# Turning the relative-value sums of an attention layer inside SBUF instead of over DRAM and TensorE

## The chip, the cores and the metric

The kernel runs on one core of a Trainium2 chip. The time is the device time of one execution in microseconds (us). Before the change it is 2808.07 us, the median of 3 runs (2802.43 to 2817.08). Engines are named as the profile names them: PE (TensorE matmuls) and PEld (its weight loads), DVE (VectorE), ACT (ScalarE), POOL (GpSimd), and SP, the engine that issues most DMAs. L875 is line 875 of the kernel.

## What is computed

Two layers act on x (64 batches, 128 rows, 128 columns), each with cross-attention to a context of 77 rows per batch and a mixture of 8 experts. The change touches the attention of layer 1, which has 16 heads of 8 columns and learned relative positions. Cut to what matters:

```python
scores = einsum('bhqd,bhkd->bhqk', q, k) + einsum('bhqd,qkd->bhqk', q, rel_key_table[ids])
attn   = softmax(scores / sqrt(8))
out    = einsum('bhqk,bhkd->bhqd', attn, v)
out    = out + einsum('bhqk,qkd->bhqd', attn, rel_value_table[ids])   # the relative values' sums
x      = x + tanh(g) * (out.reshape(B, S, H) @ Wo + bo)
# then the experts: x = x + tanh(g') * sum_e combine[e] * relu(x @ W1[e])**2 @ W2[e]
```

The second addend of `out` has a matrix of its own for every row q, since `rel_value_table[ids]` depends on q and k. The kernel therefore computes it for one q at a time, over all heads and batches of a group together. This leaves the sums with the 8 columns d on partitions, while everything else of `out` has the rows q on partitions. The sums must be turned before they can be added.

## The kernel before

**Stages.** Layer 0 comes first, then layer 1. Layer 1 works through 16 groups of 4 batches. Group 0 is done as two halves of 2 batches (nb = 2), the other 15 with nb = 4. `run` makes one step for each group, in which several generators are woven together by `weave`:

- `l1_project` (prj1) for the next group: loads x and the context (L692, L694), normalises x in place (L109 to L119, tile xg), transposes it (px, L703), projects q, k, v (L710, L712) and sends q and k through DRAM (dq and dk out at L141 and L146, qst and kst back at L726 and L738).
- `l1_relate` (rel1) for the next group: 256 small matmuls (L770), copied out by ACT (L776), written to DRAM as ra (L777) and read back in another layout as rq (L790).
- `l1_attend` (att1) for this group: 16 units, each with 4 score matmuls (L815), the addition of rq (L817, DVE), the row maximum (L818, DVE), its subtraction (L819, POOL), 4 transposes (L827), the exponential into the tile rel (L828, ACT) and 4 matmuls with the values (L835). Every four units a batch's result is turned by four PE transposes (L845) and copied into avt, with q on partitions (L846). After the units, 128 matmuls for the relative values (L875, two instructions each in the trace) fill four PSUM banks, each copied to rvs (L879, DVE).
- `l1_out` (out1) for the group before: completes `out` and multiplies it with Wo (L907, L909, L913, L915).
- the route (L929 to L953) and a share of the experts, `tape`, which fills the rest of the step: per expert 12 matmuls into pz (helper lines L156 to L158), Relu, square, a split in two parts (ACT L979 to L986, DVE L981, POOL L987), and 6 matmuls into py. Before each py the expert's weights are spread over the partitions by a matmul into pb (L599), which shares one PSUM bank with py. DVE reads py at L610 or L613 (tile ys) and frees that bank; L614 adds ys to acc, on DVE or on POOL.

**Where the change is.** At the end of `l1_attend`, rvs holds, for each block j of 32 partitions, 8 columns d on the first 8 partitions, and (head, batch, 32 rows q) along the free dimension. Four DMAs write it to DRAM as rd (L883) and one reads it back as rp with (d, head) on partitions and (batch, q) free (L885). In `l1_out` PE transposes rp (L899, one for each batch, PSUM tile po1), DVE adds it to avt (L901), DVE takes the reciprocal of the denominators (L902), and POOL multiplies (L903). Then come the transposes po2 (L907).

**What sets the order.** `PLAN` gives each generator a stretch of its step, from 0 to about 1, and some a priority; the number of parts given with the generator spreads its parts over that stretch. The compiler's scheduler then reorders the instructions of each engine by its own estimate of when they can run. On the chip each engine runs its list strictly in that order, so a waiting instruction holds up everything behind it on its engine. rvs and rp share one buffer (tag rvs), and av, o1 and oT share two (tag av).

Of the kernel before, what the change touches and what calls it, by code (L numbers as in the profile page):

```python
# [10 lines left out]
F32 = mybir.dt.float32  # L11
# [3 lines left out]
ALU = mybir.AluOpType  # L15
# [4 lines left out]
B, S, D = 64, 128, 128  # L20
KL = 77
NH = 16
HD = 8
# [18 lines left out]
def weave(tc, streams):  # L42
# [20 lines left out]
PLAN = dict(  # L63
    out=(0, 0.2, 2000),
    wei=(0, 0.7, 0),
    max=(0.2, 0.95, 1000),
    fea=(0.2, 0.6, 1000),
    out1=(0.25, 0.4, 600),
    att1=(0.1, 0.95, 0),
    rel1=(0.37, 0.93, 0),  # L70
    relT=(0.6, 0.9, 500),
# [4 lines left out]
    attE=(0, 0.35, 500),  # L76
    tE=(0.1, 1.1, 0),
    prjT=(0, 0.55, 1000),
    attL=(0.1, 0.4, 500),
# [16 lines left out]
class Net:  # L96
# [695 lines left out]
        s["rqs"][b] = rq.rearrange("q (j g) k -> q g j k", j=4)  # L792

    def l1_attend(self, s, nb):
        nc, a, dp = self.nc, self.ap, self.dp
        qst, kst, va = s["qst"], s["kst"], s["va"]
        C = NH * nb
        nq = 512 // C

        rel = self.rel  # L800
        rqs = s["rqs"]


        avt = a.tile([128, nb, NH, HD + 1], F32, tag="avt", bufs=2, name="avt")
        relg = rel.rearrange("k q (j g) b e -> k g b j q e", j=4)

        def scores(b, hg):

            m = a.tile([128, 4], F32, tag="mx", bufs=3, name="mx")
            sc = a.tile([128, 4, KL], F32, tag="sc", bufs=2, name="sc")  # L810
            r = slice(64 * (b // 2), 64 * (b // 2) + 48)
            sp = self.sbank().rearrange("p (j k) -> p j k", j=4)
            for j in range(4):
                h = 4 * j + hg
                nc.tensor.matmul(sp[:, j, :KL], lhsT=qst[r, h, b % 2, :], rhs=kst[r, h, b % 2, :], start=True, stop=True,  # L815
                                 tile_position=(r.start, 0))
            nc.vector.tensor_tensor(sc, sp[:, :, :KL], rqs[b][:, hg], ALU.add)  # L817
            nc.vector.tensor_reduce(m, sc, AX.X, ALU.max)  # L818
            nc.gpsimd.tensor_tensor(sc, sc, m.unsqueeze(2).to_broadcast([128, 4, KL]), ALU.subtract)  # L819
            return sc  # L820

        def expo(b, hg, sc):
            st = self.pST.tile([128, 4, 128], F32, tag="ST", name="ST")
            for j in range(4):

                r = 128 if j < 3 else KL
                nc.tensor.transpose(st[:r, j, :], sc.rearrange("q j k -> q (j k)")[:, j * KL : j * KL + r], self.ident)  # L827
            nc.scalar.activation(relg[:KL, hg, b], st[:KL].rearrange("k j (q e) -> k j q e", e=2), AF.Exp,  # L828
                                 scale=1.0 / math.sqrt(HD))

        def weigh(b, hg):
            for j in range(4):

                n = (b * NH + 4 * j + hg) * (HD + 1)
                nc.tensor.matmul(self.avp[32 * j : 32 * j + 32, hg, :], lhsT=va[:, n : n + 32],  # L835
                                 rhs=relg[:, hg, b, j, :], start=True, stop=True, tile_position=(0, 32 * j))
            if hg == 3:
                av = a.tile([128, 4, S], F32, tag="av", bufs=2, name="av")
                nc.scalar.copy(av, self.avp)
                turns.append((b, av))  # L840

        def turn(b, av):
            pt = self.sbank()
            for g in range(4):
                nc.tensor.transpose(pt[:, g * 128 : (g + 1) * 128], av[:, g, :], self.ident)  # L845
            nc.vector.tensor_copy(avt[:, b].rearrange("q (j g) r -> q g j r", j=4),  # L846
                                  pt.rearrange("q (g j r) -> q g j r", g=4, j=4)[:, :, :, : HD + 1])

        turns = []
        parts = [(b, hg) for b in range(nb) for hg in range(4)]  # L850
        sc = {}
        ahead = self.rqb - 1
        for b in range(len(rqs), min(nb, ahead)):
            self.l1_fetch(s, b)
        for n in range(len(parts) + 2):
            if n % 4 == 0 and ahead <= n // 4 + ahead < nb:
                self.l1_fetch(s, n // 4 + ahead)
            if n < len(parts):
                sc[n] = scores(*parts[n])
            if 0 <= n - 1 < len(parts):  # L860
                expo(*parts[n - 1], sc.pop(n - 1))
            if turns:
                turn(*turns.pop())
            if n >= 2:
                weigh(*parts[n - 2])
            yield
        turn(*turns.pop())

        rvs = a.tile([128, C, 32], F32, tag="rvs", bufs=1, name="rvs")
        for t0 in range(0, 32, nq):  # L870
            pr = self.sbank()
            for n in range(nq):
                for j in range(4):
                    q = 32 * j + t0 + n
                    nc.tensor.matmul(pr[32 * j : 32 * j + 32, n * C : (n + 1) * C],  # L875
                                     lhsT=self.rv[:, 127 - q : 131 - q, :].rearrange("k n d -> k (n d)"),
                                     rhs=rel[:, q // 2, :, :, q % 2], start=True, stop=True,
                                     tile_position=(0, 32 * j))
            nc.vector.tensor_copy(rvs[:, :, t0 : t0 + nq], pr.rearrange("p (n c) -> p c n", n=nq))  # L879
            yield  # L880
        rd = dp.tile([HD, C, 4, 32], F32, tag=f"rd{nb}", name="rd")
        for j in range(4):
            nc.sync.dma_start(out=rd[:, :, j, :], in_=rvs[32 * j : 32 * j + HD])  # L883
        rp = a.tile([128, nb * S], F32, tag="rvs", bufs=1, name="rp")
        nc.sync.dma_start(out=rp, in_=rd.rearrange("d (h b) j t -> (d h) (b j t)", h=NH))  # L885
        s["rp"], s["avt"] = rp, avt

    def l1_out(self, g, b0, nb, s):
        nc, pm, a = self.nc, self.pmisc, self.ap
        avt, rp = s["avt"], s["rp"]  # L890
        if b0 == 0:
            self.x3n = self.fp.tile([128, 4, 128], F32, tag="x1", bufs=3, name="x3")
        x3 = self.x3n[:, b0 : b0 + nb, :]
        nc.sync.dma_start(out=x3, in_=self.x2d[g, :, b0 : b0 + nb, :])
        nc.gpsimd.tensor_tensor(x3, x3, self.bo.unsqueeze(1).to_broadcast([128, nb, 128]), ALU.add)

        pt = pm.tile([128, 512], F32, tag="misc", name="po1")
        for b in range(nb):
            nc.tensor.transpose(pt[:, b * 128 : (b + 1) * 128], rp[:, b * S : (b + 1) * S], self.ident)  # L899
        o = a.tile([128, nb, NH, HD], F32, tag="av", bufs=2, name="o1")  # L900
        nc.vector.tensor_tensor(o, pt[:, : nb * 128].rearrange("q (b d h) -> q b h d", b=nb, d=HD), avt[:, :, :, :HD], ALU.add)  # L901
        nc.vector.reciprocal(avt[:, :, :, HD], avt[:, :, :, HD])  # L902
        nc.gpsimd.tensor_tensor(o, o, avt[:, :, :, HD].unsqueeze(3).to_broadcast([128, nb, NH, HD]), ALU.mult)  # L903
        yield
        pt = pm.tile([128, 512], F32, tag="misc", name="po2")
        for b in range(nb):
            nc.tensor.transpose(pt[:, b * 128 : (b + 1) * 128], o[:, b].rearrange("q h d -> q (h d)"), self.ident)  # L907
        oT = a.tile([128, nb * S], F32, tag="av", bufs=2, name="oT")
        nc.scalar.copy(oT, pt[:, : nb * S])  # L909
        yield  # L910
        pf = pm.tile([128, 512], F32, tag="misc", name="pf")
        for b in range(nb):
            nc.tensor.matmul(pf[:, b * 128 : (b + 1) * 128], lhsT=oT[:, b * S : (b + 1) * S], rhs=self.wo,  # L913
                             start=True, stop=True)
        nc.vector.scalar_tensor_tensor(x3, pf[:, : nb * 128].rearrange("p (b d) -> p b d", b=nb), self.tg[:, 1:2], x3,  # L915
                                       ALU.mult, ALU.add)
        if b0 + nb == 4:
            self.xs[self.ng + g] = self.x3n
        yield
# [124 lines left out]
    def run(self, ngroups):  # L1044
        tc, nc = self.tc, self.nc
# [26 lines left out]
        for k in range(nun + 2):  # L1072
            w = []
# [12 lines left out]
            if k == 1:  # L1086
                with tc.issue_after(self.last_dma.ins):
# [15 lines left out]
                   (self.route(ngroups - 1), 6, *PLAN["rt0"]),  # L1103
                   (self.l1_project(*h0, s1), 8, *PLAN["prjT"]),
                   (self.l1_relate(h0, s1), 7, *PLAN["relT"])], 27, PLAN["t0"])
        self.step([(self.l1_attend(s1[h0], 2), 13, *PLAN["attL"]),
                   (self.l1_project(*h1, s1), 8, *PLAN["prjL"]),
                   (self.l1_relate(h1, s1), 7, *PLAN["relL"])], self.parts(ngroups) - self.done, PLAN["t0"])
        while self.f0_open:
# [1 line left out]
        for k in range(1, ngroups + 3):  # L1111
# [12 lines left out]
                acm, self.ap = self.pool("a1", side="right")  # L1124
                self.weights(4)
            if k == 1:
                w.append((self.l1_attend(s1[h1], 2), 13, *PLAN["attL"]))
            elif k - 1 < ngroups:
                w.append((self.l1_attend(s1[k - 1, 0, 4], 4), 23, *PLAN["att1" if k < ngroups else "attE"]))
            if k < ngroups:  # L1130
                w.append((self.l1_project(k, 0, 4, s1), 8, *PLAN["prj1"]))
                w.append((self.l1_relate((k, 0, 4), s1), 13, *PLAN["rel1"]))
# [114 lines left out]
```

## Time and profile before

| what | value |
|---|---|
| median of 3 runs | 2808.07 us |
| the profiled execution's own time | 2834.67 us |
| its span | 2833.0 us |
| mean granted PE clock | 0.936 |
| busy PE / PEld | 2404.6 us (85%) / 1650.6 us (58%) |
| busy DVE / ACT / POOL | 1922.6 (68%) / 1564.2 (55%) / 1544.8 us (55%) |
| DMA, mean | 103 GB/s; 504413 packets, 264614 of them under 512 B |
| relative values (L875), first to last start | 1467.0 to 2734.3 us |

The span runs from the first to the last instruction. "Busy" says how long an engine had something in work, not that this was needed for the end. The chain of waits follows the last instruction back to what released it, again and again; time on that chain is time that the end depends on. In the lists of waits a line such as "PE po L899 <- DMA rp<-rd" gives who stood idle before which tile and line, what ended the idle time, and then the total, the number of times and the longest. PE and PEld each have a row for the same wait.

### The profile page before, as it was taken

The page shows a single profiled execution, that of the slowest core. Times are in us where ns is not written, and L with a number is a line of the kernel's source. Part 1 is how long each engine was busy: PE and PEld are TensorE (multiplying, and loading weights), DVE is VectorE, ACT ScalarE, POOL GpSimd, SP SyncE. Part 2 cuts the span into 40 slices and gives each one's busy share as a digit, 9 for nine tenths or more (in the row PEclk, how much of TensorE's full clock was granted, in tenths as well). Part 3 has the DMA queues.
Part 4 walks back from the last instruction along what each step waited for, and adds up shares of the span by engine and source line. Part 5 has one row for each costly group of instructions (what it writes and reads, how often), then busy time and mean ns, then how long its engine had stood idle before and what let it go on. Part 6 is the DMA issues. An engine that isn't in the chain of part 4 may idle for free.

```text
span 2833.0 us, 61046 instructions
## 1 busy us (share of the span) xinstructions
PE 2404.6 (85%) x23607; PEld 1650.6 (58%) x23638; DVE 1922.6 (68%) x4054; ACT 1564.2 (55%) x3030; POOL 1544.8 (55%) x1508
## 2 busy tenths in 40 slices
PE   3688898988888988988787798898888888899887
PEld 2455665666655656656564565566656666566654
DVE  3467888887887888777775456666566566666566
ACT  2455555655555655555454455556556556566556
POOL 4445555555555555454546455555556565655556
PEclk9989999999999999999998689999999999999999
DMA  6744345434445354353144655546455666544510
GB/s 141 166 102 91 94 91 110 100 92 106 93 90 116 90 115 90 72 117 76 52 93 103 146 112 119 117 95 119 104 114 119 124 122 122 126 109 109 108 30 8
DMA packets 504413, 290.56 MB, mean 103 GB/s; under 512 B 264614, under 2 KB 480814, under 8 KB 504027
## 3 DMA queue, kind: packets, MB, share of 16 engines
q1 hardware_dynamic: 476475, 246.28, 43.7%
q10 hardware_dynamic: 27648, 40.38, 4.0%
q8 instruction: 186, 3.05, 0.5%
q14 instruction: 104, 0.85, 0.1%
HBM read 147.19 MB, written 138.60 MB: 101 GB/s over the span
## 4 chain that ended last, share of the span: by engine, by line
PE 44%; DMA 20%; DVE 18%; issue 6%; POOL 6%; SPq 3%; ACT 2%; DVEq 0%; ACTq 0%; POOLq 0%
PE ST L827 3%; PE py L156 3%; PE py L157 3%; PE py L158 3%; DMA rp<-rd 2%; PE AV L835 2%; DMA qst<-dq 2%; DMA rq<-ra 2%; DMA kst<-dk 2%; PE pg L156 2%; PE AV L376 2%; PE pu L156 2%; PE S L770 2%; DMA od<-av 2%; DVE sc L817 2%
## 5 line engine op out<-in xcount | busy, mean ns | idle before, releaser
L515 POOL TENSOR_TENSOR hl<-t,hh 128x512 fp32r<-128x512 f32 x336 | 440.5, 1316 | 359.3 <-ACT hh L514 331.5
L987 POOL TENSOR_TENSOR hl<-t,hh 128x512 fp32r<-128x512 f32 x256 | 346.8, 1367 | 212.2 <-ACT hh L986 208.8
L507 ACT ACTIVATE t<-pg 128x512 f32<-128x512 f32 x336 | 200.6, 598 | 183.8 <-PE pg L158 131.8
L819 POOL TENSOR_TENSOR sc<-sc,mx 128x308 f32<-128x308 f32 x256 | 186.6, 734 | 195.6 <-DVE mx L818 150.9
L514 ACT CAST hh<-t 128x512 fp32r<-128x512 f32 x336 | 207.4, 619 | 98.8 <-DVE t L509 45.6
L508 DVE SCALAR_TENSOR_TENSOR t<-t,pg 128x512 f32<-128x512 f32 x336 | 227.0, 677 | 42.6 <-ACT t L507 40.7
L604 ACT COPY sb<-pb 128x512 f32<-128x512 f32 x256 | 149.9, 585 | 172.6 <-PE pb L599 146.6
L509 DVE TENSOR_TENSOR t<-t,pu 128x512 f32<-128x512 f32 x336 | 227.2, 677 | 22.9 <-PE pu L158 14.4
L390 ACT ACTIVATE P<-ST 77x512 f32<-77x512 f32 x256 | 151.2, 591 | 151.1 <-PE ST L387 147.4
L828 ACT ACTIVATE rel<-ST 77x512 f32<-77x512 f32 x256 | 158.2, 618 | 129.2 <-PE ST L827 126.5
L817 DVE TENSOR_TENSOR sc<-S,rq 128x308 f32<-128x308 f32 x256 | 119.9, 472 | 158.8 <-PE ST L827 61.4
L613 DVE TENSOR_TENSOR ys<-sb,py 128x512 f32<-128x512 f32 x224 | 152.4, 681 | 89.6 <-PE py L158 85.6
L827 PE MATMUL ST<-ident,sc 128*128 128x128 f32 (+1 forms) x1024 | 176.3, 299 | 17.2 <-ACT rel L828 8.2
L156 PE MATMUL pu<-xh,wu_h 128*128 128x512 f32 x336 | 157.9, 470 | 34.5 <-DVE t L508 33.1
L986 ACT CAST hh<-t 128x512 fp32r<-128x512 f32 x256 | 156.6, 626 | 55.1 <-PE py L158 47.8
L349 DVE TENSOR_REDUCE mx<-S 128x5 f32<-128x385 f32 (+1 forms) x192 | 110.7, 578 | 107.7 <-PE S L346 107.0
L156 PE MATMUL pg<-xh,wg_h 128*128 128x512 f32 x336 | 161.1, 479 | 16.6 <-DVE t L509 16.5
L979 ACT ACTIVATE t<-pz 128x512 f32<-128x512 f32 x256 | 151.3, 597 | 25.6 <-POOL hl L987 22.4
L827 PEld LDWEIGHTS ST<-ident,sc 128*128 128x128 f32 (+1 forms) x1024 | 127.2, 153 | 57.8 <-issue 19.7
L156 PE MATMUL py<-hh,wd_h 128*128 128x512 f32 x336 | 151.4, 451 | 5.4 <-ACT sb L604 3.4
L776 ACT COPY sg<-S 128x385 f32<-128x385 f32 (+1 forms) x192 | 91.9, 516 | 107.7 <-PE S L770 105.0
L157 PE MATMUL py<-hl,wd_h 128*128 128x512 f32 x336 | 145.2, 432 | 3.5 <-POOL hl L515 3.5
(248 smaller groups left out, 6535.3 us busy)
## 6 DMA issues: line engine op xcount, KB each, us to landing
rq<-ra SPq DMA_DIRECT2D x256, 154.0 KB
qst<-dq SPq DMA_DIRECT2D x96, 384.0 KB
ra<-sg ACTq DMA_DIRECT2D x128, 192.5 KB
kst<-dk SPq DMA_DIRECT2D x96, 231.0 KB
dq<-f SPq DMA_DIRECT2D x47, 384.0 KB
od<-av SPq DMA_DIRECT2D x32, 512.0 KB
ra<-sg ACTq DMA_DIRECT2D x64, 231.0 KB
dq<-f SPq DMA_DIRECT2D x47, 256.0 KB
```

Source lines behind the costliest of these rows:

```text
L156: nc.tensor.matmul(ps, lhsT=wh, rhs=xh, start=start, stop=False)
L157: nc.tensor.matmul(ps, lhsT=wh, rhs=xl, start=False, stop=False)
L507: nc.scalar.activation(t, pg, AF.Tanh, scale=0.5)
L508: nc.vector.scalar_tensor_tensor(t, t, 1.0, pg, ALU.add, ALU.mult)
L509: nc.vector.tensor_tensor(t, t, pu, ALU.mult)
L514: nc.scalar.copy(hh, t)
L515: nc.gpsimd.tensor_tensor(hl, t, hh.bitcast(F32), ALU.subtract)
L817: nc.vector.tensor_tensor(sc, sp[:, :, :KL], rqs[b][:, hg], ALU.add)
L819: nc.gpsimd.tensor_tensor(sc, sc, m.unsqueeze(2).to_broadcast([128, 4, KL]), ALU.subtract)
L827: nc.tensor.transpose(st[:r, j, :], sc.rearrange("q j k -> q (j k)")[:, j * KL : j * KL + r], self.ident)
L828: nc.scalar.activation(relg[:KL, hg, b], st[:KL].rearrange("k j (q e) -> k j q e", e=2), AF.Exp, scale=1.0 / math.sqrt(HD))
L987: nc.gpsimd.tensor_tensor(hl, t, hh.bitcast(F32), ALU.subtract)
```

## The change

`l1_attend` no longer writes rvs to DRAM. DVE transposes it in SBUF in blocks of 32 x 32 (32 partitions by 32 columns, each block by itself). In block (j, c) the partitions hold d (8 of the 32 are used) and the columns the 32 rows q of block j, so the block turned has q on the partitions of block j and d along the free dimension. 16 columns c (128 x 512 elements) are turned at once into the tile `turned`, and the 128 x 16 x 8 useful elements are added to avt in place. That is 4 pairs of transpose and addition for nb = 4, and 2 for nb = 2: 64 pairs in all. `l1_out` loses po1, its transposes and the addition; POOL multiplies avt into o1 directly. `turned` is one more tile of tag av. rp, its share of tag rvs and the DRAM tile rd are gone. The parts of `l1_attend` go from 23 to 27 (13 to 15 for a half).

```diff
     def l1_attend(self, s, nb):
...
-        rd = dp.tile([HD, C, 4, 32], F32, tag=f"rd{nb}", name="rd")
-        for j in range(4):
-            nc.sync.dma_start(out=rd[:, :, j, :], in_=rvs[32 * j : 32 * j + HD])
-        rp = a.tile([128, nb * S], F32, tag="rvs", bufs=1, name="rp")
-        nc.sync.dma_start(out=rp, in_=rd.rearrange("d (h b) j t -> (d h) (b j t)", h=NH))
-        s["rp"], s["avt"] = rp, avt
+
+        n = 16 // nb
+        turned = a.tile([128, 16, 32], F32, tag="av", bufs=2, name="turned")
+        for h in range(0, NH, n):
+            nc.vector.transpose(turned.rearrange("q c r -> q (c r)"),
+                                rvs[:, h * nb : (h + n) * nb, :].rearrange("p c t -> p (c t)"))
+            to = avt[:, :, h : h + n, :HD]
+            nc.vector.tensor_tensor(to, to, turned[:, :, :HD].rearrange("q (h b) d -> q b h d", b=nb), ALU.add)
+            yield
+        s["avt"] = avt
 
     def l1_out(self, g, b0, nb, s):
...
-        pt = pm.tile([128, 512], F32, tag="misc", name="po1")
-        for b in range(nb):
-            nc.tensor.transpose(pt[:, b * 128 : (b + 1) * 128], rp[:, b * S : (b + 1) * S], self.ident)
         o = a.tile([128, nb, NH, HD], F32, tag="av", bufs=2, name="o1")
-        nc.vector.tensor_tensor(o, pt[:, : nb * 128].rearrange("q (b d h) -> q b h d", b=nb, d=HD), avt[:, :, :, :HD], ALU.add)
         nc.vector.reciprocal(avt[:, :, :, HD], avt[:, :, :, HD])
-        nc.gpsimd.tensor_tensor(o, o, avt[:, :, :, HD].unsqueeze(3).to_broadcast([128, nb, NH, HD]), ALU.mult)
+        nc.gpsimd.tensor_tensor(o, avt[:, :, :, :HD], avt[:, :, :, HD].unsqueeze(3).to_broadcast([128, nb, NH, HD]), ALU.mult)
...
-                w.append((self.l1_attend(s1[k - 1, 0, 4], 4), 23, *PLAN["att1" if k < ngroups else "attE"]))
+                w.append((self.l1_attend(s1[k - 1, 0, 4], 4), 27, *PLAN["att1" if k < ngroups else "attE"]))
```

The two calls for a half change from 13 to 15 in the same way. In the changed kernel the transposes are at L885 and the additions at L888; the lines of `l1_attend` before them and of `l1_out` from the reciprocal (L902) on keep their numbers.

More of the change, by code (lines that the diff above doesn't have):

```diff
@@ L794, in l1_attend @@
     def l1_attend(self, s, nb):
-        nc, a, dp = self.nc, self.ap, self.dp
+        nc, a = self.nc, self.ap
         qst, kst, va = s["qst"], s["kst"], s["va"]
@@ L880, in l1_attend @@
             yield
-        rd = dp.tile([HD, C, 4, 32], F32, tag=f"rd{nb}", name="rd")
-        for j in range(4):
-            nc.sync.dma_start(out=rd[:, :, j, :], in_=rvs[32 * j : 32 * j + HD])
-        rp = a.tile([128, nb * S], F32, tag="rvs", bufs=1, name="rp")
-        nc.sync.dma_start(out=rp, in_=rd.rearrange("d (h b) j t -> (d h) (b j t)", h=NH))
-        s["rp"], s["avt"] = rp, avt
+        n = 16 // nb
[7 more added lines that the diff above has]
+        s["avt"] = avt
     def l1_out(self, g, b0, nb, s):
         nc, pm, a = self.nc, self.pmisc, self.ap
-        avt, rp = s["avt"], s["rp"]
+        avt = s["avt"]
         if b0 == 0:
@@ L1105, in run @@
                    (self.l1_relate(h0, s1), 7, *PLAN["relT"])], 27, PLAN["t0"])
-        self.step([(self.l1_attend(s1[h0], 2), 13, *PLAN["attL"]),
+        self.step([(self.l1_attend(s1[h0], 2), 15, *PLAN["attL"]),
                    (self.l1_project(*h1, s1), 8, *PLAN["prjL"]),
@@ L1126, in run @@
             if k == 1:
-                w.append((self.l1_attend(s1[h1], 2), 13, *PLAN["attL"]))
+                w.append((self.l1_attend(s1[h1], 2), 15, *PLAN["attL"]))
             elif k - 1 < ngroups:
-                w.append((self.l1_attend(s1[k - 1, 0, 4], 4), 23, *PLAN["att1" if k < ngroups else "attE"]))
+                w.append((self.l1_attend(s1[k - 1, 0, 4], 4), 27, *PLAN["att1" if k < ngroups else "attE"]))
             if k < ngroups:
```

## The prediction

> **What bounds the kernel now.** I read the page first: PE is the fullest engine (85%), DVE has 68%, the others 55%. A share over the whole span says little, so I read layer 1 next, by tile. The transposes of rp (L899) show what they wait for:
>
> ```profile
> L899 PE MATMUL po<-ident,rp x64: 270/421/477, 1545.9 to 2750.4; 128*128 128x128 f32 x64
> ...
>   DMA rp<-rd: 130.0, 25
> ```
>
> 130.0 us counts PE and its weight loads, so PE itself stood idle for about half. PE's waits between 1800 and 2670 us, where layer 1 repeats every 78.7 us, are headed by this one:
>
> ```profile
> PE po L899 <- DMA rp<-rd: 58.4, 11, 7.1
> PE S L815 <- DVE sc L817: 11.1, 13, 1.3
> PE pp L590 <- POOL p3b L129: 10.2, 11, 1.0
> ```
>
> So 11 of the 15 steps with four batches have a hole of 58.4 / 11 = 5.3 us; the other four (near 1682, 1757, 2701 and 2749 us) have hardly any. The timeline of PE around one hole:
>
> ```profile
> 2467.47 0.60 PE L827 MATMUL ST<-ident,sc 128*128 128x128 f32 x4
> 2474.71 1.11 PE L899 MATMUL po<-ident,rp 128*128 128x128 f32 x4 [6.64 <-DMA rp<-rd]
> 2475.62 0.63 PE L599 MATMUL pb<-s,sel 128*128 128x512 bf16 x1
> 2475.69 0.99 PE L156 MATMUL pz<-xh,w1s_h 128*128 128x512 f32 x1
> ```
>
> After the hole everything on PE takes about double. The stretches say why: the granted clock (the column after POOL) is 0.58 for 5.7 us, then 1.00 again.
>
> ```profile
> 2474.70:2480.40 5.70, 5.69 (x37) 4.13 (x37) 2.18 (x5) 1.97 (x4) 3.78 (x4) 0.58 1.05 137
> 2480.40:2490.00 9.60, 9.27 (x138) 6.41 (x134) 7.03 (x20) 6.40 (x13) 5.98 (x7) 1.00 0.14 51
> ```
>
> SP's timeline shows where the detour spends its time. rd is issued at 2454.22 (four DMAs, 5.29 us); rp stands behind dq, dk, rq and x in SP's list and starts only 13 us later:
>
> ```profile
> 2454.22 5.29 SPq L883 DMA_DIRECT2D rd<-rvs  x4
> ...
> 2467.07 1.04 SPq L885 DMA_DIRECT2D rp<-rd  x1
> ```
>
> **What the change removes, for each of the 11 steps.** The hole: 5.3 us. The half clock behind it: 5.7 us at 0.58 loses 5.7 x 0.42 = 2.4 us. Four PE transposes: 0.60 us at full clock (the step at 2701.68, which has no hole); 0.55 with their overlap. Together 8.25 us. On SP 5.29 + 1.04 us of issue go, so qst, kst and rq move up. I count nothing for it: "PE S L770 <- DMA qst<-dq" is only 0.5 us in those 870 us.
>
> **What it adds.** Four pairs of transpose and addition on DVE for each step, in place of L901 (0.69 us). The trace has no DVE transpose. Its lower bound is the fastest 128x512 row from SBUF, the cast at L126 (0.42 us in the timeline); its upper bound is L614, 1.105 us on average. I take 0.65, near the 128x512 rows of 0.68 (L508, L613, L879), since a block transpose also passes every element once. The addition has 128 elements a partition and both inputs in SBUF: between 0.25 (below the copy of 144 elements, L846, 0.304) and 0.72 (L231, 256 elements, two SBUF inputs). I take 0.40. A pair is then 1.05 us (0.67 to 1.83), four pairs 4.2 us.
>
> ```profile
> L614 DVE TENSOR_TENSOR acc<-acc,ys 128x512 f32<-128x512 f32 x128 | 141.4, 1105 | 3.8
> L231 DVE TENSOR_TENSOR r_ge<-r_p 128x256 f32<-128x256 f32 x32 | 23.1, 723 | 0.5
> L846 DVE COPY avt<-S 128x144 f32<-128x144 f32 x64 | 19.4, 304 | 15.9 <-PE S L845 15.3
> ```
>
> L614 has a median of 0.692 us by its own view, so many of its executions are stretched. The Trainium skill gives a reason in "SBUF — State Buffer", section "Who interferes with whom": a VectorE instruction with two SBUF inputs contends with a GpSimd instruction that reads SBUF. L901, which goes, has one input in PSUM; the additions that come have both in SBUF, so this rule speaks against the change. Another does too: "VectorE: DVE Perf Modes", section "The three transpose paths", gives 311 ns for a VectorE transpose of 128x128 bf16. Four times that, as an estimate, is 1.24 us for 512 columns; with it the sum below would be a gain of 2 us and the time 2806. No row here shows either duration for float32.
>
> **Where the pairs stand.** The order of the built programs tells. The pairs follow the last copy of rvs in DVE's list, and behind them stands ys (L613), which frees the bank of py and pb; PE's second pb (L599) waits for it. So the pairs are on the way of PE. I count from T, the end of px (2518.3 in the cycle shown); xg lands 3.3 us later. Before, DVE's list then ran:
>
> ```profile
> 2525.75 1.28 DVE L879 COPY rvs<-S 128x512 f32<-128x512 f32 x2
> 2527.11 0.43 DVE L128 CAST f<-fq 128x512 bf16<-128x512 f32 x1
> 2529.05 0.86 DVE L817 TENSOR_TENSOR sc<-S,rq 128x308 f32<-128x308 f32 x2 [1.50 <-DMA rq<-ra]
> ...
> 2531.17 0.67 DVE L613 TENSOR_TENSOR ys<-sb,py 128x512 f32<-128x512 f32 x1
> ```
>
> ys ended at T + 13.5, and PE had been busy for 13.1 us of that.
>
> In the changed build the steps alternate between two orders. In the first, DVE has between xg and the end of ys, with the durations of before: statistics 0.87, reciprocal 0.56, aggregates 0.36, two rvs copies 1.3, a square 0.68, normalising 1.12, two casts 0.85, two rvs copies 1.36, L579 0.68, the casts of f3k 0.61 and 0.84, four copies L748 0.88, ys 0.68: 10.8. With the pairs 15.0, with 0.5 for POOL's part of f between the casts 15.5: ys ends at T + 18.8. PE's list before the second pb holds 13.8 us of work by the rows of before (py 1.4, L875 4.4, L770 1.8, L845 0.45, pz 1.4, L710 1.15, po 0.55, L815 0.5, pb 0.25, pv 0.45, py 1.4). PE so waits 18.8 - 13.8 = 5.0 us. In the second order the reciprocal, f3k's second cast and L748 stand outside: 7.2 + 4.2 after xg, ys at T + 14.7, with 9.4 us of work for PE: 5.3 us. Less the 0.4 of before, the new wait costs 4.7 us on average.
>
> Two corrections. PE's idle 1.25 us just behind ys (at 2532.3, L815 for sc) falls together with the new wait: +1.25. PE runs at 0.57 for 3 us behind it now, a loss of 1.3; behind a wait of 5 us I take the 2.4 of the hole: -1.1.
>
> **The sum.** A step with a hole gains 8.25 - 4.7 + 1.25 - 1.1 = 3.7 us; 11 of them 41. Three without a hole lose 4.7 - 1.25 + 1.1 = 4.55: -14. Around 1560 us, where the buffers are exchanged, the second half's rd and rp are waited for with little else on PE (5.25 us), and POOL's clearing of rel (6.92 us) starts behind them; from rvs to the multiplication it took 11.3 us (1562.3 to 1573.6), with two pairs about 3. Part lies beside the relate matmuls: -7. At the end the last rp is no longer waited for, but the route ends last there (L899 waits 0.67 for ACT): -3. In all 41 - 14 + 7 + 3 = 37 us: 2834.67 - 37 = 2797.7. That execution stands 0.9% over the median of 2808.07; times 0.9906 this is 2771 us. With the pair at its ends, 0.67 and 1.83, 60 pairs move this by -23 and +47 us: 2748 and 2818.
>
> Cover: the additions' end releases POOL's multiplication (1.16) and po2. In PE's list po2 stands behind the second pb and 6 to 12 py, 3 us or more, so this is hidden; were po2 put ahead of them, it would cost about 1.2 us a step. Behind POOL's multiplication stand the hl of the experts (L987), which PE needs only behind the second pb.
>
> **Rivals.**
> *The pairs are hidden*: DVE absorbs them because POOL and ACT leave it gaps elsewhere, and PE never waits for ys. Then 11 x 8.25 + 10 = 101 us go: 2734 of the profile, 2708 us. For it: DVE is busy for 47 of 79 us in a cycle. Against it: ys stands directly behind them.
> *Another transfer ends last*: in the first order the last L770 stand behind L875, so ra is written later and the first scores (L817) wait for rq, 8.6 us behind the last L770 as now (2520.4 to 2529.05). That would be T + 19, level with ys; if rq slips by 3.7 us more, the steps gain nothing: about 2812 us.
> *Slower, DVE's pairs become the bound*: every microsecond on a pair costs 60 us (15 x 4). The 37 us are gone at 1.05 + 37 / 60 = 1.67 us a pair. If the transpose takes two passes (2 x 0.68 = 1.36) and the addition waits for POOL as L231 does (0.72), a pair is 2.08: +62 us, 2834.67 + 25 = 2860, and 2833 us.
> That the change doesn't do what it says is out: the built program has 64 transposes and no rd, rp or po1.
>
> **Chances.** Forecast (2735 to 2794) 0.48; hidden (below) 0.15; another transfer 0.17; slower 0.20. A difference within 0.5% can't be told from no change here, so faster 0.63, same 0.17, slower 0.20. The range of 8 in 10 reaches into both sides, 2712 to 2826.
>
> **What will show it.** Right: no wait on rp; a wait of PE at L599 for DVE ys of 4 to 5 us each step; pairs near 1.05 us; the cycle at 75 us instead of 78.7; the clearing of rel some 7 us earlier. Wrong: a transpose over 1.2 us, the additions stretched past 0.7 us, or PE waiting for rq (L815 for sc) longer than for ys.

## The result, and the profile after

The changed kernel takes 2824.95 us (median of 20 runs, 2811.20 to 2839.40); the kernel before takes 2812.69 us (20 runs, 2802.43 to 2828.70). The ratio is 1.0045, 95% interval 1.0027 to 1.0063: slightly slower, where 0.9868 was forecast. The profiled execution of after took 2812.68 us, near the lower end of its runs; that of before (2834.67 us) was above all of its own. Of the 22 us between their spans 20 lie ahead of the first px (1406.9 and 1387.2 us), in layer 0, where the change has no instruction. So the two traces are compared step by step, not by their spans.

On the page PE's busy time hardly moves (2404.6 to 2400.8 us) and DVE's grows from 1922.6 to 1970.0 us: the pairs are 65.9 us, and L901 is gone. The detour is gone. PE's waits of after between 1800 and 2670 us (total, times, longest) have no line for rp, but this one has taken the first place:

```profile
PE S L815 <- DVE sc L817: 24.2, 6, 6.1
PE pb L599 <- DVE ys L613: 10.5, 17, 1.1
PE py L156 <- ACT sb L604: 9.0, 14, 1.0
```

The wait of L599 for ys, which the prediction expected at 4 to 5 us a step, is 10.5 us in all. In its place PE waits for the scores. DVE's waits in the same stretch name the cause, a transfer:

```profile
DVE sc L817 <- DMA rq<-ra: 38.7, 7, 9.0
```

Before, the same line was

```profile
DVE sc L817 <- DMA rq<-ra: 9.2, 8, 1.5
```

The pairs themselves cost what was estimated (duration minimum, median, maximum in ns):

```profile
L885 DVE STREAM_TRANSPOSE turned<-rvs x64: 675/711/715, 1460.3 to 2708.6; 128x512 f32<-128x512 f32 x64
L888 DVE TENSOR_TENSOR avt<-avt,turned x64: 260/291/734, 1461.5 to 2709.3; 128x128 f32<-128x128 f32 x64
```

From px (L703) to the next px a step of before takes 78.8 us, each like the other. After alternates: 86.6, 70.6, 86.3, 70.3, 86.8, 70.7 us. The mean of eight is 78.6: what the hole cost has come back inside the long steps. One of them, which starts at 2161.0, shows how. Three lines of PE's timeline (start, duration, engine, line) give the step's px, the last relate matmuls, and the first scores that need what they computed:

```profile
2160.99 0.66 PE L703 MATMUL px<-ident,xg 128*128 128x128 f32 x4
...
2172.48 0.25 PE L770 MATMUL S<-tst,qst 48*32 48x77 bf16 x4 [1.22 <-issue]
...
2174.41 0.45 PE L815 MATMUL S<-kst,qst 48*128 48x77 bf16 x8
```

SP's timeline of the same step:

```profile
2169.66 3.29 SPq L141 DMA_DIRECT2D dq<-f  x3
2176.25 1.23 SPq L726 DMA_DIRECT2D qst<-dq  x2
2177.58 11.31 SPq L790 DMA_DIRECT2D rq<-ra  x11
```

ACT's, DVE's and PE's, each from its own timeline of the same stretch:

```profile
2172.78 0.86 ACT L776 COPY sg<-S 128x385 f32<-128x385 f32 x2 [3.46 <-PE S L770]
```

```profile
2187.64 0.87 DVE L817 TENSOR_TENSOR sc<-S,rq 128x308 f32<-128x308 f32 x2 [5.96 <-DMA rq<-ra]
```

```profile
2188.17 0.69 PE L815 MATMUL S<-kst,qst 48*128 48x77 bf16 x8 [3.67 <-DVE sc L817]
```

The last relate matmuls end at 2172.73. ACT copies the last pieces of both halves out only then, and the ra that the first scores hang on has landed by 2176.7 (the trace's semaphores tell of each landing). SP has qst ahead of rq in its list. The two qst land at 2181.5 and 2184.0, and only behind them the four rq that the first scores wait for (issued at 2177.58 to 2180.66): the first at 2184.9, the last at 2187.5, 26.5 us behind px. Where qst goes out behind rq, in the short steps of after and in before, the first rq lands 2.8 to 3.7 us after its issue; here it takes 7.3. The scores have stood ready since 2174.9. DVE waits 5.96 us, PE behind it 3.67 us, and then the clock falls: in the next 10.3 us it is 0.83 (the column after POOL in the stretches' view).

```profile
2188.10:2198.40 10.30, 9.56 (x52) 6.79 (x52) 7.70 (x14) 5.93 (x11) 7.40 (x7) 0.83 1.00 165
```

### The profile page after: what moved, and what is told of

It reads as the page before. It is cut to its first block, busy times and chain, and to the rows that moved or that the text cites. A ratio compares the mean times of both kernels' runs of the same rounds, so it can differ in the third digit from the quotient of the medians.

```text
span 2810.7 us, 60925 instructions
## 1 busy us (share of the span) xinstructions
PE 2400.8 (85%) x23574; PEld 1636.5 (58%) x23574; DVE 1970.0 (70%) x4165; ACT 1566.9 (56%) x3030; POOL 1556.2 (55%) x1508
## 5 line engine op out<-in xcount | busy, mean ns | idle before, releaser
L817 DVE TENSOR_TENSOR sc<-S,rq 128x308 f32<-128x308 f32 x256 | 120.0, 474 | 153.7 <-DMA rq<-ra 52.9
L827 PE MATMUL ST<-ident,sc 128*128 128x128 f32 (+1 forms) x1024 | 166.0, 286 | 23.9 <-POOL sc L819 11.5
L827 PEld LDWEIGHTS ST<-ident,sc 128*128 128x128 f32 (+1 forms) x1024 | 118.0, 145 | 66.7 <-POOL sc L819 28.3
L614 POOL TENSOR_TENSOR acc<-acc,ys 128x512 f32<-128x512 f32 x96 | 128.5, 1338 | 45.6 <-DVE ys L613 44.2
```

## The experiments

The theories were: 1, the pairs on DVE are on PE's way; 2, not the pairs but the new order of the lists eats the gain; 3, any wait that is taken away comes back elsewhere. The table holds all runs. Each ratio is to runs of before that were taken along with it on the same chip; the median of before was 2812.7 us with after, 2827.2 with e1 to e4, 2822.6 with e5 to e8 and 2834.1 with e9 to e12, so kernels of different rounds are compared by way of before. "Step" is the mean of eight steps around 1850 to 2560 us from px to px in the profiled execution, "idle" PE's idle time in one, "half" the time in one at half clock, all in us.

| kernel | parts | ratio to before (95%) | step | idle | half |
|---|---|---|---|---|---|
| before | 23, detour | 1 | 78.8 | 9.5 | 8.1 |
| after | 27, pairs | 1.0045 (1.0027 to 1.0063) | 78.6 | 8.7 | 6.4 |
| e1 | 23, pairs in one part | 0.9813 (0.9791 to 0.9835) | 74.8 | 7.4 | 1.3 |
| e2 | 23, no pairs | 0.9758 (0.9739 to 0.9777) | 74.3 | 5.2 | 4.3 |
| e3 | 23, pairs in the next step | 0.9797 (0.9774 to 0.9820) | 75.3 | 7.6 | 2.1 |
| e4 | 27, detour | 1.0355 (1.0330 to 1.0380) | 86.3 | 13.6 | 15.4 |
| e5 | 27, pairs in one part | 1.0074 (1.0045 to 1.0104) | 81.0 | 9.6 | 9.0 |
| e6 | 27, rq in long rows | 1.0140 (1.0109 to 1.0171) | 81.4 | 10.3 | 9.8 |
| e7 | 23, transposes twice | 0.9877 (0.9843 to 0.9910) | 76.7 | 6.4 | 7.6 |
| e8 | 25, pairs in one part | 1.0138 (1.0102 to 1.0174) | 80.2 | 9.5 | 8.5 |
| e9 | 23, pairs as in after | 0.9800 (0.9770 to 0.9830) | 75.1 | 7.4 | 2.1 |
| e10 | 27, no wait for rq | 0.9732 (0.9699 to 0.9765) | 72.5 | 3.7 | 0.4 |
| e11 | 25, detour | 1.0244 (1.0210 to 1.0278) | 84.6 | 10.8 | 14.9 |
| e12 | 23, pairs late, relate first | 0.9770 (0.9746 to 0.9794) | 74.9 | 5.8 | 0.9 |

**e1, the pairs in one part, 23 and 13 parts.**

```diff
             nc.vector.tensor_tensor(to, to, turned[:, :, :HD].rearrange("q (h b) d -> q b h d", b=nb), ALU.add)
-            yield
...
-                w.append((self.l1_attend(s1[k - 1, 0, 4], 4), 27, ...
+                w.append((self.l1_attend(s1[k - 1, 0, 4], 4), 23, ...
```

> The changed kernel with its four pairs in one part of l1_attend, and 23 and 13 parts as before the change. The built program then has one order of PE for every step in place of two in turn. Theory 1 (the pairs on DVE are on PE's way): the pairs are all there, so nothing moves: 2825 us within 6. Theory 2 (not the pairs but the new order of the lists, with long and short steps in turn and the relate matmuls cut up, eats the gain): the order of two steps in turn goes, most of its 1.9 us a step of lost PE work with it: 28 us less, about 2797. Theory 3 (the hole at rp was slack that others needed anyway; a wait taken away at one place returns elsewhere): 2825 within 12.

Measured 0.9813: more than theory 2 asked for (2797 would be 0.994), and against theories 1 and 3. Every step is now of one kind, 73.4 to 76.5 us. The view of tile rq (what ended DVE's idle time ahead of L817, total and times), where after has "DMA rq<-ra: 52.9, 11", says:

```profile
  PE ST L827: 33.3, 32
  PE S L815: 15.8, 16
...
  DMA rq<-ra: 1.1, 1
```

**e9, the change with nothing but its numbers of parts put back.** It separates e1's two edits.

```diff
-        self.step([(self.l1_attend(s1[h0], 2), 15, *PLAN["attL"]),
+        self.step([(self.l1_attend(s1[h0], 2), 13, *PLAN["attL"]),
...
-                w.append((self.l1_attend(s1[h1], 2), 15, *PLAN["attL"]))
+                w.append((self.l1_attend(s1[h1], 2), 13, *PLAN["attL"]))
...
-                w.append((self.l1_attend(s1[k - 1, 0, 4], 4), 27, ...
+                w.append((self.l1_attend(s1[k - 1, 0, 4], 4), 23, ...
```

> The changed kernel with one thing put back: the numbers of parts (23 and 13). The four pairs keep their separate parts. Theory P (numbers of parts): ratio to before 0.975 to 0.987, steps of one kind of 75 us. Theory Y (the separate parts): 1.00 to 1.01.

0.9800, as theory P said. So the swap itself is a gain of 2.0%, and the numbers of parts give back 1.0045 - 0.9800 = 2.45%, 69 us of 2813. The longest of PE's waits in e9 between 1800 and 2670 us, DVE's wait for rq there, and SP's timeline of a step that starts at 2167.3:

```profile
PE pb L599 <- DVE ys L613: 22.1, 27, 1.6
PE pz L156 <- ACT t L979: 10.7, 10, 1.4
PE S L815 <- DVE sc L817: 10.6, 12, 3.2
```

```profile
DVE sc L817 <- DMA rq<-ra: 3.7, 2, 3.4
```

```profile
2177.15 0.40 SPq L141 DMA_DIRECT2D dq<-f  x1
2178.63 5.76 SPq L790 DMA_DIRECT2D rq<-ra  x8
2184.49 0.74 SPq L141 DMA_DIRECT2D dq<-f  x1
```

Here rq goes out 11.3 us behind px (16.6 in the long step of after), ahead of qst, at 0.72 us an issue. Its first four transfers have landed 18.3 us behind px. The score matmuls that need it come 21 us behind px and their addition 22: they find it landed. The wait for ys, twice that of after, is the dearest and costs 2 us a step.

**e5, the numbers of parts without the separate parts.** e1 with 27 and 15.

```diff
-                w.append((self.l1_attend(s1[k - 1, 0, 4], 4), 23, ...
+                w.append((self.l1_attend(s1[k - 1, 0, 4], 4), 27, ...
```

> The kernel with all four pairs in one part, but with the change's numbers of parts (27 and 15). Theory P (the numbers of parts do the harm: they set the parts of l1_attend 15% closer together, so that the next scores come up before their rq has landed): as the changed kernel, ratio to before 1.00 to 1.01, with long and short steps in turn. Theory Y (the four separate parts with the pairs do it, by what the weaving puts between them): as the kernel with the pairs in one part and 23, ratio 0.98.

1.0074, within what theory P gave. Its list of waits is after's: L815 for sc 25.9 us, L817 for rq 37.7 us. The steps go from 71.3 to 87.3 us.

**e4, the numbers of parts on the kernel before**, with its detour (23 to 27, 13 to 15 in the same three lines).

> The kernel before, with its detour over DRAM, and only the numbers of parts of the change (27 and 15 in place of 23 and 13). The steps then go in two kinds in turn here too. Theory 1: no pairs, so 2813 us within 6. Theory 2: the order alone costs what the changed kernel loses, 20 to 35 us: 2833 to 2848. Theory 3: 2813 within 12, with waits in other places.

1.0355: the numbers alone cost even more than theory 2 asked. PE's longest waits between 1800 and 2670 us are the hole and two new ones:

```profile
PE po L899 <- DMA rp<-rd: 43.6, 10, 5.2
PE ST L827 <- POOL sc L819: 32.0, 17, 4.3
PE pb L599 <- DVE x L579: 14.8, 10, 2.4
```

DVE's L817 waits for rq as long as in after (38.8 us, 10 times), but beside the hole at rp, so that PE waits for its sc (L815) only 8.0 us. The 32.0 us at ST stand in the middle of the steps, some 52 us behind px. So the numbers cost the detour too, but by other waits. Against this kernel, at equal numbers, the changed one is 1.0045 / 1.0355 = 0.970.

**e8 and e11, 25 parts**, with the pairs in one part and with the detour (in both the one line for steps of four batches).

> The kernel with all four pairs in one part, with 25 parts in place of 23 or 27 for the steps of four batches. Theory P: the closer the parts stand the earlier the scores come: between the two, ratio 0.985 to 1.0. Theory L (the time follows the chance result of the scheduler's order, no trend in the number): outside this, below 0.98 or above 1.005.

> The kernel before, with its detour over DRAM, with 25 parts in place of 23 for the steps of four batches (13 for the halves). If any number other than 23 costs some per cent with the detour too: between 1.005 and 1.04 (27 and 15 cost 3.55%). If the loss is bound to 27 and 15: 0.995 to 1.005. With the pairs in place of the detour 25 measured 1.0138: if the detour's hole costs its 1.9% at every number, this kernel is at 1.033.

With the pairs 25 gives 1.0138, worse than 27: no trend in the number, as theory L said. With the detour it gives 1.0244, less than e4's 1.0355 and less than the 1.033 of a fixed price for the hole. The pairs are faster than the detour at each number: 0.980 (23), 1.0138 / 1.0244 = 0.990 (25), 0.970 (27). And 25 has its own first wait, so rq is not all that binds. e8, PE between 1800 and 2670 us:

```profile
PE pb L599 <- DVE ys L613: 34.4, 21, 3.8
PE S L815 <- DVE sc L817: 25.9, 21, 4.2
```

What follows the number in all the traces is the distance from the last relate matmul to the first score matmul behind it, in which ra is written and rq read back. Over nine steps of each kernel from 1780 us on it is 5.7 to 14.5 us with 23 parts (before about 7.0), 2.6 to 3.1 with 25 (two steps of e8 have 6.9 and 8.4), and 0.8 to 2.5 with 27. DVE's wait for rq between 1800 and 2670 us is at most 9.2 us with 23, 20.7 and 39.2 with 25 (e8, e11), and 37.7 to 67.4 with 27 (e10, where nothing waits for rq, is left out). The times don't follow in that order: the new lists bring other waits too.

**e10, nothing waits for rq, 27 and 15 parts.**

```diff
-            nc.vector.tensor_tensor(sc, sp[:, :, :KL], rqs[b][:, hg], ALU.add)
+            nc.vector.tensor_tensor(sc, sp[:, :, :KL], self.wqkv.rearrange("p n c -> p (n c)")[:, : 4 * KL].rearrange("p (j k) -> p j k", j=4), ALU.add)
```

> The changed kernel with its numbers of parts (27 and 15), where the addition to the scores takes a constant tile in place of rq (so the relative keys are left out of the scores); rq is still computed, written to DRAM and read back, but nothing waits for it. The long kind of step (74 relate instructions behind px) is still there in every second step. Theory R (the wait for rq and the half clock behind it make the closer parts slow): the wait is gone, the kernel gets 40 to 60 us faster than the changed one, ratio 0.983 to 0.99. Theory O (the order itself): ratio 1.0 or over.

0.9732, more than theory R's 0.983, although the long order is still in every second step (80 relate instructions behind px, and the next scores 1.7 us behind the last of them, as in after). PE's waits between 1800 and 2670 us are small all over, and the clock is hardly ever halved (0.4 us a step):

```profile
PE ptf L929 <- DVE ln_xn L119: 8.3, 7, 6.7
PE pz L156 <- ACT t L979: 5.7, 10, 2.3
PE ST L827 <- ACT rel L828: 4.9, 7, 1.1
```

The lists of this kernel are ordered anew (without rq the scheduler places the scores elsewhere), so the whole 3.1% isn't the price of the wait. That the long order must be slow (theory O) is refuted.

**e6, rq in long rows**, an attempt on the same wait by way of the transfer.

```diff
-                                   in_=s["rd"][b // 2, x].rearrange("(h e) n k -> e n h k", e=2)[b % 2])
+                                   in_=s["rd"][b // 2, x].rearrange("(e c) (g m) k -> e (c g) m k", e=2, m=16)[b % 2])
```

> The changed kernel with rq read from DRAM in long rows (4928 bytes at a stretch in place of 308). The same bytes are moved, but from other places, so the scores have wrong addends. The built order has the long kind of step each time, with 74 of the relate instructions' 256 behind px. If the late rq and the half clock behind that wait make the long steps long (theory R), the wait of L815 for sc and of L817 for rq goes, and with 1.4 us of idle time and 2.5 us of clock a step: 15 x 3.9 = 58 us less than the changed kernel, ratio 0.98 to 0.985. If the long order itself costs it (theory O: the same instructions in an order that PE, ACT and DVE run worse), every step is as long as the long ones (86): 15 x 8 = 120 us more than the changed kernel, ratio 1.04 or over.

1.0140, neither theory's number: the edit did not take the wait away. L817 waits for rq 67.4 us, 11 times, between 1800 and 2670 us. All steps are long ones, 79.8 to 82.6 us. SP's timeline, in a step that starts at 1944.4:

```profile
1961.17 1.23 SPq L726 DMA_DIRECT2D qst<-dq  x2
1962.51 9.41 SPq L790 DMA_DIRECT2D rq<-ra  x12
```

The issues are quicker (0.78 us), but start 18 us behind px, again behind qst. qst lands 22.0 and 24.6 us behind px and the four rq at 25.1 to 27.1; L817 begins at 1971.60, 27 us behind px. So what makes rq late is when it may start and what stands ahead of it, more than the length of its rows.

**e2, no pairs at all**, 23 and 13 parts: from `n = 16 // nb` to the last `yield` of `l1_attend` left out.

> The changed kernel without the pairs: the relative values' sums are computed and copied to rvs, but left out of the output; 23 and 13 parts. Theory 1: 4.0 us of DVE a step leave PE's way, 15 steps, about 60 us less than the changed kernel: 2765. Theory 2: the time follows the order of PE's list, which here goes in two kinds of steps again, but with 48 to 64 of the relate matmuls behind px as in the kernel with the pairs in one part: within 10 us of that kernel. Theory 3: 2825 within 12, with another wait in place of the pairs.

0.9758, 0.55% or 15 us less than e1: theory 2 held (10 us) better than theory 1 (60). In e1 the pairs take 97 us of DVE (64 transposes of 0.70 and additions of 52 us in all); with 15 us, about a sixth of that is on the path. PE's wait for ys falls from 21.3 us in e1 to 4.8. The lists of e2 are ordered anew, so the 15 us are not the price of the pairs alone.

**e7, each transpose twice**, on e1.

```diff
+            nc.vector.transpose(turned.rearrange("q c r -> q (c r)"),
+                                rvs[:, h * nb : (h + n) * nb, :].rearrange("p c t -> p (c t)"))
```

> The kernel with the pairs in one part and 23 and 13 parts, each transpose done twice: DVE has 64 x 0.69 = 44 us more, or 2.8 us a step. If the pairs lie wholly on PE's way, as the prediction priced them (60 us for each microsecond of a pair): 41 us more than with one transpose, ratio 0.995. If they are mostly hidden, as the 15 us between the kernels with and without pairs say (a quarter of their time): 10 us more, ratio 0.985.

0.9877, 18 us more than e1 for 44 us of DVE: between the two, 0.4 us for each microsecond. Its steps are not of one kind (70.6 to 84.1 us), so the figure is a rough one.

**e3, the pairs in `l1_out` of the next step**, ahead of the reciprocal, and **e12**, the same with `rel1=(0.37, 0.93, 300)` in `PLAN`.

> The changed kernel with the pairs moved from the end of l1_attend into l1_out of the next step, ahead of the reciprocal, 23 and 13 parts. PE's order is that of the kernel with all pairs in one part. Theory 1: the pairs no longer stand ahead of ys, so the wait of PE for ys goes: some 30 to 60 us less than with the pairs in one part. Theory 2: the same as with the pairs in one part, within 6 us. Theory 3: the same, within 12.

> The pairs moved into l1_out of the next step (23 and 13 parts), and the relate matmuls given priority 300, so that all but the last 60 instructions stand where they did and these a little ahead of the scores that need rq. Theory R: rq lands no later than in the kernel with late pairs, where nothing waits for it any more, so nothing moves: ratio 0.975 to 0.985. Theory O: another order, anything from 0.97 to 1.02.

e3 is at 0.9797, the same as e1 and e9 within their intervals. It doesn't show that the place of the pairs is of no matter: the scheduler put them where they were. In a step of e3 the transposes start 22.8, 25.9, 30.3 and 33.6 us behind px, in e9 23.0, 26.2, 30.5 and 33.8. The wait for ys stays (2 us a step); its longest, 1.5 us, is right behind the last pair. e12 is the fastest that computes everything, 0.9770; its interval meets those of e1, e3 and e9, so it is at least as good and not shown better.

## Why the prediction was wrong

**The hole and its clock: right.** No wait on rp is left. In e9, where no new hole comes in its place, the time at half clock falls from 8.1 to 2.1 us a step. That e9's step is 75.1 us, where the forecast said 75 instead of 78.7, is chance: e9 has another order than the two that were priced, and its wait for ys is 2 us, not 5.

**The pair: right.** 1.05 us was taken (0.65 + 0.40); 0.711 + 0.291 was measured at the medians, so two small errors cancel. The estimate of 1.24 us for the transpose alone, from the Trainium skill's figure for bf16 ("VectorE: DVE Perf Modes", section "The three transpose paths"), was too high by three quarters.

**The wait for ys: wrong in size.** In the long step at 2161 ys ends at T + 18.9 (T + 18.8 was forecast), but PE waits only 0.85 us for it. PE's list ahead of the second pb took not 13.8 us but 18: about 15 of work and 3 of other waits (1.43 for the projected k on ACT, 1.22 of issue, 0.39 for v). So PE's sum was too short: 10.5 us in 870 in place of 4.7 a step. DVE's was right in its total by luck: 15.0 us of work and 0.5 of waiting were put between xg and the end of ys, and 12.9 of work and 2.8 of waiting were measured.

**"8.6 us behind the last L770 as now": the step that failed.** It put rq level with ys at T + 19 in the first order, and the rival "another transfer ends last" at 0.17. The last L770 ends 11 us behind T, about as counted, but the addition that needs rq starts 14.9 us later (2172.73 to 2187.64). The 8.6 us of before were not a chain from that L770: the ra that this rq needs had been issued at 2518.34, 2 us ahead of it, and qst went out 30 us behind px. In after both halves' ra go out last, which takes 4.0 us until the landing; qst ahead on SP takes 0.9 more until the first rq is issued, the four issues start over 3.1 us (1.4 before), and the fourth lands 6.9 us after its start (5.5 before), behind the transfers of qst. The prediction saw that qst moves up and counted nothing for it. rq lands 7 us behind ys, where 3.7 was the point from which nothing is gained. Both orders had been priced at nearly the same gain; measured are 86.6 us for this one and 70.6 for the other, whose first scores find rq landed. The rival had the late rq and a price (2812 us; 2825 was measured), at a chance of 0.17.

**The numbers of parts: the term that was missing.** The change was priced as pairs in place of a detour, in the two orders that the built program showed, but the orders were taken as given. They come from 27 and 15: the same 18 parts of units stand 15% closer (0.85 / 27 of the step apart in place of 0.85 / 23), the scores come up 13 us behind px in place of 21 (e9), 1.7 us behind the last relate matmul in place of 10, and rq is not there for them. In before they came 10 us behind px, but the relate ended 2.8 us behind it: the distance counts, not the time of either. With the pairs the numbers cost 2.45% (e9) and 2.6% (e5 against e1), and e10 shows the loss gone with the wait for rq. With the detour they cost 3.55% (e4), there by other waits.

**The slower rival: refuted as put.** It was 60 us for each microsecond on a pair. e2 and e7 measured 15 us for all pairs, and 18 us for 0.69 us more on each.

**Transition and end.** The four steps around the exchange of the buffers took 217.9 us before and 203.7 after, 14 us less (7 were forecast), of which the next two steps gave back 8. The end, from the last px, took 236.9 and then 248.4 us: 11 more, not 3 less.

**What stays open.** By the table the 3.5 us between a step of e9 and one of after are 1.3 of idle time and 4.3 at half clock, which cost 2.1 (an estimate: half the work is done in them). Not all of that clock is behind rq: of the 51 us at half clock in after's eight steps 17 stand at the wait for rq, and 27 at the end of the long steps, where PE has no single gap over 1 us. No run kept the order of after and took away the wait for rq alone, so whether that end follows from it isn't settled. At 25 parts another wait leads. And the change itself gains less than its waits: from before to e9 idle time and clock fall by 5.1 us a step, the step by 3.7; no run explains the difference.

## What to carry to other kernels

Where a scheduler weaves the work, a change of one operation and a change of the numbers that pace it are two changes: build and time them apart, above all when the second came along only because the first has more parts. Follow the transfers that are started by the instructions that move, through the issuing queue, to who waits for them; here, against e9, rq went out 5 us later (16.6 and 11.3 us behind px) and behind qst, for scores that came 8 us earlier (13 and 21), and that was the new hole. And price an instruction on a busy engine only after the other engine's list up to the meeting point has been summed with its own waits.

## What the runs showed of the hardware

The fp32 transpose of 128 x 512 in blocks takes 0.70 us, as much as a copy of that shape (L879, 0.68). The addition that follows depends on its neighbour. In e9 its median is 1.02 us, 3.5 times that of after:

```profile
L888 DVE TENSOR_TENSOR avt<-avt,turned x64: 271/1022/1359, 1485.6 to 2694.4; 128x128 f32<-128x128 f32 x64
```

Sorted by what POOL does meanwhile, 38 of e9's additions lie for over half of their time beside a POOL instruction and take 1.31 us in the median; the other 26 take 0.275. Each of the 38 ends 0.14 to 0.16 us after the POOL instruction that was running when it began, however long that still took. This agrees with the contention of which the Trainium skill warns in "SBUF — State Buffer", section "Who interferes with whom"; this case's trace gives it a price of 1.0 us. Yet e9, with pairs of 1.5 us on average, is 2.45% faster than after, with pairs of 1.03: DVE had the room.

The time of an execution goes with its clock: of after's 20 runs the fastest (2811.20 us) had a mean granted PE clock of 0.944, the slowest (2839.40) of 0.932. Two profiles can so differ by 1% with nothing changed.
